# A semaphore for each of the 48 places of gathered rows in a message-passing kernel

## The chip, the cores and the metric

The kernel runs on one core of a Trainium2 chip. The metric is the device time of one execution in microseconds (us), lower is better; of several executions the median is given. A profiled execution gives a span, which runs from the first to the last instruction, and a trace of every instruction, DMA packet and semaphore event.

The engines are named as in the profile: PE is TensorE (PEld its weight loads), DVE is VectorE, ACT is ScalarE, POOL is GpSimd and SP is SyncE. A "q" behind a name (POOLq, DVEq, ACTq, SPq) is the engine's instruction queue, in which waits and DMA issues stand.

## The reference

There are 50,000 nodes with 160 features and 1,650,000 edges, sorted by their destination `dst`; `src` is in no order. For each edge the source node's row is fetched and combined with four numbers of the edge; the messages are summed at the destination, multiplied by small matrices, added to the node, and normalized:

```python
ss, vv = (s[src], v[src])                       # rows of x, by source
...
m = jnp.concatenate([out0, out1.reshape(-1, 3 * MUL1)], axis=1)
m_agg = jax.ops.segment_sum(m, dst, num_segments=n)
hs = m_agg[:, :MUL0] @ Ws * LIN_S
hv = jnp.einsum('nui,uw->nwi', m_agg[:, MUL0:].reshape(n, MUL1, 3), Wv) * LIN_V
h = jnp.concatenate([hs, hv.reshape(n, 3 * MUL1)], axis=1)
return x + jax.nn.relu(h)
...
x = _layernorm(x + _L0_gnn_ref(x, edge_attr_4, ...), axis=-1)
```

The messages are linear in the edge's numbers and in the source's row, so the kernel first sums the rows weighted by each of the four numbers and applies the merged matrices once for each node.

## The kernel before

**Units, groups, pairs, chunks.** 128 edges are a unit: one row of `x` (640 bytes) in each of the 128 partitions. Six units make a group (`G`), whose destinations lie within 32 neighbouring nodes; two groups make a pair (`PG`), so a pair has 12 units; 20 groups (`SG`), ten pairs, make a chunk. The main loop is written out over all 1,044 pairs.

**Fetching the rows.** The rows of a unit are fetched in one of two ways.

- Most come by an indirect DMA that POOL issues (line 468 in `gather`). It reads 128 row numbers, one column of the table `si`, and fetches the 128 rows into one of the 12 places of a tile `xg` (`rows[j]` is `xg[:, j, :]`). The pool `rowp` has four such tiles, 4 x 12 = 48 places, used in turn. POOL issues 12,230 of these gathers, in the order of the edges, and does next to nothing else.
- From the seventh chunk on ACT fetches the rows of two units in each chunk, and from the ninth on SP those of one (class `Fetcher`): 128 DMAs of one row each, into tiles `xscalar` and `xsync`. These DMAs increase a semaphore that the kernel itself allocates for the tile (`then_inc`), and the matmul that reads the tile waits for that semaphore by an explicit `wait_op`.

**What the matmuls do.** DVE makes a tile `ha` for each pair (line 486): for each edge of the pair its place among the 32 nodes, times its four numbers. PE then runs one matmul for each unit (line 511 in `group_sums`), `ha` by the fetched rows, and sums six units in `ps`. DVE turns the sums (line 527) and adds them into a ring of nodes (line 536). When a block of 128 nodes is complete PE multiplies it by the merged matrices (line 831) and DVE and ACT finish the nodes.

**What sets the order.** PE, DVE, ACT and SP run their instructions in the order in which the program is written; POOL's gathers are in the order of the pairs. The waits are put in by the framework that the kernel is written in. It knows which instruction writes and reads each tile. For the gathers it has eight semaphores, which the rows of the program call `DMASW0_49` to `DMASW7_49` (lanes, below): the gathers take them in turn, each adds 16 to its lane when it has landed, and before a gather takes a lane it waits until the lane's gather before, eight gathers earlier, has landed. The matmul of a unit waits for the lane of its gather. The first gather into a tile `xg` also waits for PE (`PE_49`), until the matmuls that read the tile's rows four tiles earlier are done, and at the start of a chunk for DVE (`DVE_49`), which writes the chunk's table `si` (line 426). That write in turn waits for all eight lanes, since older gathers read the table's buffer.

Of the kernel before, what the change touches and what calls it, by code (L numbers as in the profile page):

```python
# [67 lines left out]
PG = 2  # L68
# [16 lines left out]
def plan(n_nodes, n_edges):  # L85

    nblk = 125
    assert n_nodes % nblk == 0
    assert W == FB
    nb = n_nodes // nblk  # L90
    again = 9

    per_unit = P * n_nodes / n_edges
    group = max(g for g in range(1, 17)
                if g == 1 or (g + 0.2) * per_unit + 1 + 5 * math.sqrt(g * per_unit * per_unit / P) <= W)
    head = math.ceil(min(HEAD, n_edges / (group * P)) / SG) * SG
    eh = head * group * P
    row = group * P * 3 // 2 + math.floor(per_unit * group * 3 / 2 * (1 - n_nodes / n_edges))
    assert row * n_nodes / n_edges + 5 * math.sqrt(row * n_nodes / n_edges / 16) < KM

    far = math.ceil(6 * math.sqrt(n_edges) / 2 * n_nodes / n_edges) + 2
    rows = math.ceil((n_edges - eh) / row) + 2
    ngroups = math.ceil((n_edges - n_nodes + eh * n_nodes / n_edges + far) / (group * P))
    assert eh + (rows - 1) * row - n_nodes + eh * n_nodes / n_edges - far >= ngroups * group * P
    units = P * math.ceil(max(math.ceil(n_edges / P) + again - 1, math.ceil((eh + rows * row + 1) / P)) / P)
    return nblk, nb, again, group, units, ngroups, row, head, rows, far
# [3 lines left out]
def tile_gnn_resnorm(ctx: ExitStack, tc: tile.TileContext, x, src, dst, attr, W1, W2, W3, W4, W5, Ws, Wv, out, n_edges):  # L110
    nc = tc.nc
    N = x.shape[0]
    NBLK, NB, GA, G, NU, NG, L, NH, NR, FAR = plan(N, n_edges)
# [95 lines left out]
    def near(g):  # L209
        p = g * G * P  # L210
        return p / degree if p <= EH else EH / degree + (p - EH) / (degree - 1)
# [6 lines left out]
    for g0, g1 in parts:  # L218
        t = min((near(g) / N for g in range(g0, g1 + 1)), key=lambda t: abs(t - 0.5))
# [14 lines left out]
    with tc.tile_pool(name="once", bufs=1) as once, tc.tile_pool(name="raw", bufs=2) as rawp, \  # L234
# [182 lines left out]
        def place(cast_):  # L417
# [40 lines left out]
            begun.append(nc.vector.tensor_reduce(extremes[:, 1, s:s + 1], rel[:, :n], axis=AX.X, op=ALU.max))  # L458
            placed[s] = si, rel, pk[:, :, us]

        def gather(s, placed, u, n):

            xg = rowp.tile([P, PG * G, D], F32, name="xg")
            rows = [fetched.pop((s, u + j), None) for j in range(n)]
            for j in range(n):
                if rows[j] is None:
                    rows[j] = xg[:, j, :], None, None, None
                    nc.gpsimd.indirect_dma_start(  # L468
                        out=xg[:, j, :], out_offset=None, in_=x,
                        in_offset=bass.IndirectOffsetOnAxis(ap=placed[0][:, u + j:u + j + 1], axis=0))  # L470
            return rows

        idle, sent = [], []
# [22 lines left out]
        def fresh(kind):  # L496
            written[kind].append([])

        def wrote(kind, ins):
            ws = written[kind]  # L500
            for old in ws[-3] if len(ws) > 2 else []:
                tc.declare_no_dep(ins.ins, old, reason="its reader has waited for it")
            ws[-1].append(ins.ins)
            return ins

        def group_sums(p, rows, ha):

            ps = psA.tile([P, PG, D], F32, name="ps")
            fresh("ps")
            for j, (xr, sem, count, key) in enumerate(rows):  # L510
                mm = nc.tensor.matmul(ps[:, j // G, :], ha[:, j].rearrange("p k w -> p (k w)"), xr,  # L511
                                      start=j % G == 0, stop=j % G == G - 1)
                if key:
                    mm.wait_op(sem, count, "sem-ge")
                    tc.declare_no_dep(mm.ins, group=key, reason="their own semaphore is waited for")
                    tc.declare_fence(mm.ins, group=key)
                if j % G == 0:
                    wrote("ps", mm)
                else:
                    written["ps"][-1].append(mm.ins)  # L520
                yield ps
# [22 lines left out]
        def row_start(r):  # L544

            lo, hi = (math.floor(r * L * (1 - 1 / degree)) - 2 * FAR - 2, math.ceil(r * L * (1 - 1 / degree)) + 2 * FAR + 2)
            return (max(lo, 0), hi if r else 0), (max(math.floor((EH + r * L) / degree) - FAR - 2, 0),
                                                  math.ceil((EH + r * L) / degree) + FAR + 2)
# [234 lines left out]
        def own_blocks(k):  # L783

            if min((k + 1) * S, N) <= row_start(0)[1][0]:
                return []
            return [list(range(b, min(b + BP, nblocks))) for b in range(k * SB, min((k + 1) * SB, nblocks), BP)]
# [196 lines left out]
        for i in range(npacks):  # L984
# [3 lines left out]
            own = next((k for k in range(NSEG) if min((k + 1) * S, N) > row_start(i * RP)[1][0] and own_blocks(k)), NSEG - 1)  # L988
# [22 lines left out]
        for p, (s, g, ng) in enumerate(pairs):  # L1011
# [5 lines left out]
            if p % per == 0 and s + 1 < NSC:  # L1017
                after_pair(p + 1, do_cast, s + 1)
                after_pair(p + 2, do_place, s + 1)
                if s + 2 == NSC:  # L1020
                    after_pair(p + 4, examine_all)
                    after_pair(p + 6, read_flags)
            rows = gather(s, placed[s], (g - s * SG) * G, ng * G)
            for j, ps in enumerate(group_sums(p, rows, has.pop(p))):
                if j == 1 and turning:
                    turn_sums(*turning)
                    turning = None
                if j == 3 and p + 1 < len(pairs):
                    s1, g1, ng1 = pairs[p + 1]
                    has[p + 1] = spread(placed[s1], (g1 - s1 * SG) * G, ng1 * G)  # L1030
                work(1.0)
                if p % per == FBEGIN and not j:
                    begun_at = p
                    for f in fetchers:
                        f.begin(s)
                for f in fetchers:
                    if f.left:
                        f.deal((p - begun_at + (j + 1) / (ng * G)) / per)
                if packs and p >= START:
                    when = p + (j + 1) / (ng * G)  # L1040
                    todo = math.ceil(len(packs[0]) * min(1, (when - began) / max(1, due[0] - began)))
                    for step in packs[0][done:todo]:
                        if step:
                            step()
                    done = max(done, todo)
                    if done == len(packs[0]):
                        packs.pop(0), due.pop(0)
                        done, began = 0, when
# [35 lines left out]
    with tc.tile_pool(name="up", bufs=1) as up, tc.tile_pool(name="us", bufs=2) as us, tc.For_i(0, once_more, 1):  # L1084
# [3 lines left out]
        mm = up.tile([P, 2, JU], F32, name="mm")  # L1088
# [32 lines left out]
        f = up.tile([PB, CB], F32, name="f")  # L1121
# [12 lines left out]
    with tc.tile_pool(name="edges2", bufs=2) as ep, tc.tile_pool(name="ops2", bufs=2) as op, \  # L1134
            tc.tile_pool(name="node2", bufs=1) as np_, tc.tile_pool(name="psA2", bufs=2, space=PSUM) as psA, \
            tc.tile_pool(name="psF2", bufs=1, space=PSUM) as psF:
        with tc.For_i(0, blocks, 1) as b:
# [5 lines left out]
            with tc.For_i(u0, u1, GA) as u:  # L1143
# [10 lines left out]
                xg = op.tile([P, GA, D], F32, name="xg2")  # L1154
# [71 lines left out]
```

## Time and profile before

| | |
|---|---|
| median of 3 runs | 15441.45 us |
| the three runs | 15405.63, 15441.45, 15442.74 us |
| the profiled execution | 15404.57 us, its span 15402.8 us |
| granted TensorE clock, mean | 0.578 of full speed |
| busy: PE / PEld / DVE / ACT / POOL | 10200.3 / 6755.8 / 7650.5 / 171.3 / 11597.4 us |
| HBM traffic over the span | 87 GB/s |

How to read what follows. A row of a view of groups gives the line, the engine, the operation, what is written and read, and the count; then the busy time and the mean duration of one in ns; then the idle time of the engine just before these instructions, with what ended it. For an indirect DMA on POOL the busy time is that in which POOL generates the transfer's descriptors; the transfer itself runs later on the 16 DMA engines. "issue" means that the profile shows nothing that the engine waited for. A row of the timeline gives the start and the duration in us, then the same names, and in brackets the idle time before it.

### The profile page before, as it was taken

The page shows a single profiled execution, that of the slowest core. Times are in us where ns is not written, and L with a number is a line of the kernel's source. Part 1 is how long each engine was busy: PE and PEld are TensorE (multiplying, and loading weights), DVE is VectorE, ACT ScalarE, POOL GpSimd, SP SyncE. Part 2 cuts the span into 40 slices and gives each one's busy share as a digit, 9 for nine tenths or more (in the row PEclk, how much of TensorE's full clock was granted, in tenths as well). Part 3 has the DMA queues.
Part 4 walks back from the last instruction along what each step waited for, and adds up shares of the span by engine and source line. Part 5 has one row for each costly group of instructions (what it writes and reads, how often), then busy time and mean ns, then how long its engine had stood idle before and what let it go on. Part 6 is the DMA issues. An engine that isn't in the chain of part 4 may idle for free.

```text
span 15402.8 us, 171527 instructions
## 1 busy us (share of the span) xinstructions
PE 10200.3 (66%) x28971; PEld 6755.8 (44%) x28972; DVE 7650.5 (50%) x12616; ACT 171.3 (1%) x273; POOL 11597.4 (75%) x12243
## 2 busy tenths in 40 slices
PE   3666666666666666666666666666666666666666
PEld 3444444444444444444444444444444444444444
DVE  8455355445535543563465355445634553554333
ACT  0000000000000000000000000000000000000000
POOL 7777777777777777777777777777777777777777
PEclk6655555555555555555555555555555555555555
DMA  3333333333333333333333333333333333333333
GB/s 83 100 81 94 91 81 85 97 88 83 92 94 81 84 96 91 81 85 98 87 83 91 93 82 84 97 88 82 86 98 87 81 88 93 81 86 85 86 81 75
DMA packets 906388, 1346.70 MB, mean 87 GB/s; under 512 B 291294, under 2 KB 680162, under 8 KB 902614
## 3 DMA queue, kind: packets, MB, share of 16 engines
q0 software_dynamic: 587040, 1002.66, 27.9%
q1 hardware_dynamic: 266794, 315.98, 6.7%
q10 hardware_dynamic: 51440, 17.04, 0.6%
q14 instruction: 883, 7.23, 0.2%
q8 instruction: 231, 3.78, 0.1%
HBM read 1263.28 MB, written 71.42 MB: 87 GB/s over the span
## 4 chain that ended last, share of the span: by engine, by line
POOL 53%; issue 23%; DMA 19%; PE 5%; DVE 1%; POOLq 0%
POOL xg L468 53%; DMA xg<-in_x,si 19%; PE ps L511 4%; PE phb L831 0%; DVE ha L486 0%; DVE ring L822 0%; DVE ring L536 0%; DVE sums L527 0%; DVE xr L818 0%; DVE hot L483 0%; DVE prow L697 0%; DVE ring L781 0%; DVE pri L692 0%; DVE spots L590 0%; DVE marks L690 0%
## 5 line engine op out<-in xcount | busy, mean ns | idle before, releaser
L468 POOL DMA_INDIRECT xg<-in_x,si x12230 | 11593.9, 948 | 3782.0 <-issue 3511.0
L511 PE MATMUL ps<-xg,ha 128*128 128x160 f32 x24460 | 9452.6, 501 | 5187.1 <-DMA xg<-in_x,si 4721.5
L511 PEld LDWEIGHTS ps<-xg,ha 128*128 128x128 f32 x24460 | 5773.0, 292 | 8629.5 <-DMA xg<-in_x,si 7467.8
L527 DVE STREAM_TRANSPOSE sums<-ps 128x320 f32<-128x320 f32 x1044 | 536.4, 514 | 6840.4 <-PE ps L511 6817.2
L486 DVE TENSOR_TENSOR ha<-hot,pk 128x1536 f32<-128x1536 f32 x1044 | 1830.5, 1753 | 35.9
L831 PE MATMUL phb<-BWk,ring 128*128 128x160 f32 (+1 forms) x3910 | 1256.1, 418 | 0.0
L831 PEld LDWEIGHTS phb<-BWk,ring 128*128 128x128 f32 (+1 forms) x3910 | 1027.4, 296 | 0.0
L536 DVE TENSOR_TENSOR ring<-ring,sums 128x160 f32 x2087 | 684.6, 328 | 340.1 <-issue 203.6
L483 DVE TENSOR_TENSOR hot<-bank,rel 128x384 f32<-128x384 f32 x1044 | 573.4, 549 | 12.6 <-DMA xt<-in_x 10.8
L697 DVE COPY_PREDICATED prow<-marks,prow 128x2370 f32<-128x2370 int32 (+5 forms) x198 | 548.6, 2771 | 1.1
L822 DVE STREAM_TRANSPOSE ring<-xr 128x1280 f32<-128x1280 f32 x188 | 467.4, 2486 | 6.5
L697 DVE COPY_PREDICATED pra<-marks,pra 128x1580 f32<-128x1580 int32 (+5 forms) x198 | 377.0, 1904 | 0.0
L818 DVE TENSOR_TENSOR xr<-xr,bank 128x1280 f32<-128x1280 f32 x188 | 278.9, 1484 | 6.6 <-DVE bank L817 0.2
L186 DVE SCALAR_TENSOR_TENSOR y<-phb,xt 128x320 f32<-128x320 f32 x196 | 95.5, 487 | 240.6 <-PE phb L831 240.3
L196 ACT ACTIVATE rstd<-mv,eps_t 128x2 f32<-128x2 f32 x196 | 58.0, 296 | 14076.2 <-DVE mv L191 13455.5
L533 DVE TENSOR_TENSOR ring<-ring 128x196 f32<-128x196 f32 (+20 forms) x485 | 149.0, 373 | 1.8
L511 PE MATMUL ps<-xscalar,ha 128*128 128x160 f32 x392 | 140.4, 460 | 0.0
L202 DVE TENSOR_SCALAR o<-y,mv,rstd 128x160 f32<-128x160 f32 x391 | 131.3, 377 | 7.5
L694 DVE COPY_PREDICATED_SCALAR hit<-marks,none 128x395 int32 (+5 forms) x198 | 129.8, 656 | 7.0
L781 DVE MEMSET ring<- 128x1280 f32 (+1 forms) x98 | 119.3, 1218 | 22.6 <-issue 22.6
L190 DVE BATCH_NORM_STATS2 st<-y 128x6 f32<-128x160 f32 x391 | 121.7, 311 | 6.7
L695 DVE COPY_PREDICATED hit<-marks,pri 128x395 int32<-128x395 int32 (+5 forms) x198 | 118.2, 597 | 6.9
(352 smaller groups left out, 2173.6 us busy)
## 6 DMA issues: line engine op xcount, KB each, us to landing
xscalar<-in_x ACTq DMA_DIRECT2D x25088, 0.6 KB
xsync<-in_x SPq DMA_DIRECT2D x12288, 0.6 KB
xg<-in_x,si POOLq DMA_INDIRECT x12230
xr<-in_x SPq DMA_DIRECT2D x187, 640.0 KB
r<-edges SPq DMA_DIRECT2D x100, 384.0 KB
edges<-prow SPq DMA_DIRECT2D x1330, 27.8 KB
xt<-in_x SPq DMA_DIRECT2D x195, 160.0 KB
out<-o SPq DMA_DIRECT2D x195, 160.0 KB
```

What stands on the lines that cost most here:

```text
L202: nc.vector.tensor_scalar(o[:n, i], y[:n, i], mv[:n, i, 0:1], rstd[:n, i:i + 1], op0=ALU.subtract, op1=ALU.mult)
L468: nc.gpsimd.indirect_dma_start(out=xg[:, j, :], out_offset=None, in_=x, in_offset=bass.IndirectOffsetOnAxis(ap=placed[0][:, u + j:u + j + ...
L483: idle[:] = [nc.vector.tensor_tensor(hot[:, :n], slotsP[:, 0:W].unsqueeze(1).to_broadcast([P, n, W]), rel[:, u:u + n].unsqueeze(2).to_broa ...
L486: nc.vector.tensor_tensor(ha[:, :n], hot[:, :n].unsqueeze(2).to_broadcast([P, n, NK, W]), pk[:, :, u:u + n].rearrange("p k u -> p u k").un ...
L511: mm = nc.tensor.matmul(ps[:, j // G, :], ha[:, j].rearrange("p k w -> p (k w)"), xr, start=j % G == 0, stop=j % G == G - 1)
L527: nc.vector.transpose(at[:, :ng], ps[:, :ng].rearrange("p g (b f) -> p g b f", f=FB))
L533: nc.vector.tensor_tensor(ring[k][:, b, :past], ring[k][:, b, :past], ring[k - 1][:, b, S:S + past], op=ALU.add)
L536: nc.vector.tensor_tensor(here, here, at[:, i], op=ALU.add)
L697: nc.vector.copy_predicated(what[:n, a:e], mi[:, r].unsqueeze(2).to_broadcast([n, e - a, what.shape[2]]), what[:n, a + d:e + d])
L818: nc.vector.tensor_tensor(xr[:, :nq], xr[:, :nq], sumP[:, :nq].unsqueeze(2).to_broadcast([P, nq, D]), op=ALU.mult)
L822: nc.vector.transpose(ring[k][:, :, c0:c0 + nq * W].rearrange("p b (w q) -> p q b w", q=nq), xr[:, :nq].rearrange("p q (b f) -> p q b f", ...
L831: wrote("misc", nc.tensor.matmul(ph[:nb], ring[k][:, i, c0:c0 + nb], BWk[:, i, :], start=i == 0, stop=i == ND - 1))
```

## The change

Each of the 48 places gets a semaphore of its own, `filled0_0` to `filled3_11`. A gather adds 16 to the semaphore of its place when it has landed, is taken out of the framework's lanes (`no_tile_sem_insts`), and its matmul waits for that semaphore. The framework is told that this matmul needs no further wait for the gather (`declare_no_dep`) and that the gather is known to have landed once the matmul runs (`declare_fence`). ACT's and SP's rows had this arrangement before and keep it.

```diff
+        filled = [[tc.alloc_semaphore(f"filled{t}_{j}") for j in range(PG * G)] for t in range(4)]
+        gathers = [[0] * (PG * G) for t in range(4)]
+        begun_tiles = [0]
+
         def gather(s, placed, u, n):
 
             xg = rowp.tile([P, PG * G, D], F32, name="xg")
             rows = [fetched.pop((s, u + j), None) for j in range(n)]
+            t = begun_tiles[0] % 4
+            begun_tiles[0] += 1
             for j in range(n):
                 if rows[j] is None:
-                    rows[j] = xg[:, j, :], None, None, None
-                    nc.gpsimd.indirect_dma_start(
+                    part = nc.gpsimd.indirect_dma_start(
                         out=xg[:, j, :], out_offset=None, in_=x,
                         in_offset=bass.IndirectOffsetOnAxis(ap=placed[0][:, u + j:u + j + 1], axis=0))
+                    gathers[t][j] += 1
+                    key = f"gather{begun_tiles[0]}_{j}"
+                    part.then_inc(filled[t][j], 16)
+                    tc.no_tile_sem_insts.add(part.ins.name)
+                    tc.add_to_no_dep_group(key, part.ins)
+                    rows[j] = xg[:, j, :], filled[t][j], 16 * gathers[t][j], key
             return rows
...
-                if key:
-                    mm.wait_op(sem, count, "sem-ge")
-                    tc.declare_no_dep(mm.ins, group=key, reason="their own semaphore is waited for")
-                    tc.declare_fence(mm.ins, group=key)
+                mm.wait_op(sem, count, "sem-ge")
+                tc.declare_no_dep(mm.ins, group=key, reason="its own semaphore is waited for")
+                tc.declare_fence(mm.ins, group=key)
```

No instruction that computes or moves data is added, removed or reordered on any engine; the waits in front of them differ. Two places show it. Lines behind the edit carry higher numbers in the changed kernel: the gather of line 468 is line 473 there, the matmul of line 511 is line 522.

POOL in the middle of the program, the gathers into one tile `xg` from the first of a chunk on and the first of the next tile. Before:

```order
L468 DMA xg<-in_x,si 128x160 [waits DMASW3_49,DVE_49,PE_49]
L468 DMA xg<-in_x,si 128x160 [waits DMASW4_49]
L468 DMA xg<-in_x,si 128x160 [waits DMASW5_49]
L468 DMA xg<-in_x,si 128x160 [waits DMASW6_49]
L468 DMA xg<-in_x,si 128x160 [waits DMASW7_49]
L468 DMA xg<-in_x,si 128x160 [waits DMASW0_49]
L468 DMA xg<-in_x,si 128x160 [waits DMASW1_49]
L468 DMA xg<-in_x,si 128x160 [waits DMASW2_49]
L468 DMA xg<-in_x,si 128x160 [waits DMASW3_49]
L468 DMA xg<-in_x,si 128x160 [waits DMASW4_49]
L468 DMA xg<-in_x,si 128x160 [waits DMASW5_49]
L468 DMA xg<-in_x,si 128x160 [waits DMASW6_49]
```

The same place in the changed kernel (`x11` is eleven equal rows that follow each other):

```order
L473 DMA xg<-in_x,si 128x160 [waits DVE_49,PE_49]
L473 DMA xg<-in_x,si 128x160 x11
L473 DMA xg<-in_x,si 128x160 [waits PE_49]
L473 DMA xg<-in_x,si 128x160 x11
L473 DMA xg<-in_x,si 128x160 [waits PE_49]
```

Every wait for a lane is gone; the waits for PE at a tile's first gather and for DVE at a chunk's first gather stand where they stood, and each waits for the same matmul as before.

DVE in the middle of the program, where it writes the table `si` of a later chunk (`rel` and `extremes` belong to the same chunk). Before:

```order
L447 STREAM_TRANSPOSE pk<-r_24905 128x4x4x32
L426 TENSOR_SCALAR si<-bank 128x120 [waits DMASW4_49,DMASW5_49,DMASW3_49,DMASW6_49,DMASW2_49,DMASW7_49,DMASW1_49,DMASW0_49]
L453 SCALAR_TENSOR_TENSOR rel<-bank,baseB 128x120
L457 TENSOR_REDUCE extremes<-rel 128x1 [waits DVE_49]
L458 TENSOR_REDUCE extremes<-rel 128x1
```

And in the changed kernel:

```order
L447 STREAM_TRANSPOSE pk<-r_24905 128x4x4x32
L426 TENSOR_SCALAR si<-bank 128x120
L453 SCALAR_TENSOR_TENSOR rel<-bank,baseB 128x120
L457 TENSOR_REDUCE extremes<-rel 128x1 [waits DVE_49]
L458 TENSOR_REDUCE extremes<-rel 128x1
```

The wait for all eight lanes is gone here too.

## The prediction

> **What bounds the kernel now.** I read the page's chain of waits first, then the groups of POOL, then the view of line 468 alone. From the page, the chain that ended last:
>
> ```profile
> POOL 53%; issue 23%; DMA 19%; PE 5%; DVE 1%; POOLq 0%
> ```
>
> From the view of POOL's groups, and from the view of line 468 (duration as minimum/median/maximum in ns, first and last start in us; then idle time before it and its count, by what ended it):
>
> ```profile
> L468 POOL DMA_INDIRECT xg<-in_x,si x12230 | 11593.9, 948 | 3782.0 <-issue 3511.0 <-PE ps L511 137.6 <-DMA xg<-in_x,si 121.8
> ```
>
> ```profile
> L468 POOL DMA_INDIRECT xg<-in_x,si x12230: 940/946/2522, 5.7 to 15379.1; - x198
> L468 POOLq EVENT_SEMAPHORE  x1040: 17/17/43, 58.8 to 15365.4; - x174
> ...
>   issue: 3511.0, 11468
>   PE ps L511: 137.6, 445
>   DMA xg<-in_x,si: 121.8, 287
> ...
>   DVE si L426: 2.9, 1
> ```
>
> POOL's gathers run from 5.7 us to 15379.1 us of a span of 15402.8, so POOL sets the pace all along: 11593.9 busy and 3782.0 idle make 15375.9. What remains is 5.7 us ahead of the first gather, which the second figure holds in part, and some 23 behind the last. The chain's 19% of DMA is no such share to be won: such a piece bridges several gathers, while POOL generates the next ones.
>
> Is the idle time a wait that can go? The timeline of POOL at the start answers it. The second to the eighth gather wait for nothing in either program, since no lane has been used yet:
>
> ```profile
> 7.08 0.95 POOL L468 DMA_INDIRECT xg<-in_x,si  x1 [0.31 <-issue]
> 8.33 0.95 POOL L468 DMA_INDIRECT xg<-in_x,si  x1 [0.30 <-issue]
> ...
> 14.58 0.95 POOL L468 DMA_INDIRECT xg<-in_x,si  x1 [0.30 <-issue]
> 15.83 0.95 POOL L468 DMA_INDIRECT xg<-in_x,si  x1 [0.30 <-issue]
> 17.08 0.94 POOL L468 DMA_INDIRECT xg<-in_x,si  x1 [0.30 <-issue]
> ```
>
> From 7.08 to 17.08 are eight gathers, 1.250 us each, and the pitch is the same with no wait (to 14.58) and with a wait for a lane that is satisfied (from 15.83). So 0.946 of generation and about 0.304 of idle time are what a gather costs without any waiting: 12,230 x 1.250 = 15287.5, nearly the whole span. Only what exceeds this can be won.
>
> PE is no second bound. In the view of waits (total us, times, longest us):
>
> ```profile
> PE ps L511 <- DMA xg<-in_x,si: 4721.5, 7053, 6.9
> PEld ps L511 <- issue: 441.7, 168, 36.8
> DVE sums L527 <- PE ps L511: 6817.2, 902, 17.2
> ```
>
> PE waits 4721.5 us for gathers, and DVE 6817.2 for PE.
>
> **The change part by part.**
>
> *The waits for lanes on POOL (removed).* A gather that lands more than about eight pitches, 10.0 us, after its start holds up the gather eight places behind it. The timeline shows it in one place, PE's row being the matmul of the gather that started at 8390.37:
>
> ```profile
> 8390.37 0.95 POOL L468 DMA_INDIRECT xg<-in_x,si  x1 [0.30 <-issue]
> 8391.62 0.95 POOL L468 DMA_INDIRECT xg<-in_x,si  x1 [0.30 <-issue]
> ...
> 8399.12 0.95 POOL L468 DMA_INDIRECT xg<-in_x,si  x1 [0.30 <-issue]
> 8402.55 0.90 PE L511 MATMUL ps<-xg,ha 128*128 128x160 f32 x2 [3.61 <-DMA xg<-in_x,si]
> 8402.76 0.94 POOL L468 DMA_INDIRECT xg<-in_x,si  x1 [2.70 <-DMA xg<-in_x,si]
> 8404.18 0.94 POOL L468 DMA_INDIRECT xg<-in_x,si  x1 [0.47 <-DMA xg<-in_x,si]
> ```
>
> The gather of 8390.37 lands some 12.1 us later, PE starts at 8402.55, and POOL, eight gathers on, at 8402.76 after 2.70 us of idle time: 2.4 more than without a wait. No later work on POOL makes that up, so it counts in full.
>
> All such stalls together: the idle time of 3782.0, less 2.9 of the first gather (it waits for `si`), less 12,229 times the idle time that no wait explains. That last figure has two ends. With 0.304, from the pitch above, 3717.6 is taken off and 61.5 us are left. With 3511.0 / 11468 = 0.306, the mean of those that the profile puts to "issue", 3744.5 is taken off and 34.6 are left; this is too little, since a wait for two semaphores is often put down to "issue". I take the middle, 0.305: 3729.8 off, **49 us** left, with 35 and 62 as the ends. The stalls put to PE belong to it: 137.6 / 445 = 0.309 each, hardly over the rest.
>
> *What takes the wait's place.* POOL's next limit is the wait for PE at a tile's first gather. Behind it stand this tile's 11 other gathers and all later ones, and PE, then DVE, would wait for those. It binds only when PE is at least 36 gathers behind, 36 x 1.25 = 45 us. The longest landing in the chain is this one:
>
> ```profile
> 8391.62 12.31 DMA xg<-in_x,si
> ```
>
> 12.31 us are ten gathers, and the longest single wait of PE's weight loads is 36.8. I take 0; the upper bound is the old stall come back, the whole 49. PE gets the late rows when it got them before and waits for those behind them less, out of 4721.5 us of slack.
>
> *More transfers at once.* After a late landing about two more gathers stand in the DMA queue than eight (ten, as above). From the page, by queue: packets, MB, share of the engines' time:
>
> ```profile
> q0 software_dynamic: 587040, 1002.66, 27.9%
> ```
>
> The gathers use 27.9% of the DMA engines' time, so the extra ones drain about three times as fast as POOL makes new ones. 0 taken; the upper bound is the first rival below.
>
> *POOL's separate wait instructions.* About 930 of its 1,040 EVENT_SEMAPHORE go, as a tile's first gather now has one wait in place of two. They take 17 ns each, 16 us at most; but the mean idle time before a gather put to PE, mostly such first ones, is 0.309 against 0.306, 3 ns more, so 930 x 3 ns = 3 us, hidden in the 0.30 otherwise. I count 0.
>
> *The waits on DVE and PE.* DVE's waits at the write of `si`:
>
> ```profile
> L426 DVEq EVENT_SEMAPHORE  x412: 21/50/50, 247.1 to 15232.3; - x138
> ```
>
> 412 x 0.05 = 21 us of DVE's queue. It lies under DVE's 6817.2 us of waiting for PE; with that cover gone it would be 21 us. On PE every matmul still waits for exactly its own gather, as before, and each matmul group for DVE: 0.
>
> **The sum.** 15402.8 - 49 = 15353.8, and 1.8 for what lies around the span (15404.57 - 15402.8): **15355 us**. With the ends it is 15342 to 15370. The profiled execution is the fastest of the four: the runs shown are 15405.63, 15441.45 and 15442.74. The 36 us between the two kinds can be more stalls at the lanes (landings a little slower, with many near the limit of 10.0 us) or 3 ns more on each of 12,230 gathers (36.7 us). In the first case the change takes them too and every run comes to 15355; in the second, two runs in three would stay at 15441 - 49 = 15392. I forecast the first, since landings of 10 to 12 us against a limit of 10.0 mean that a small delay adds up quickly.
>
> **The rivals.**
>
> *Slower: a deeper queue makes generation slower.* POOL's slowest gathers, with what DVE did beside them:
>
> ```profile
> 68.46 1.61 DVE L573 SCALAR_TENSOR_TENSOR node<-at,node 1x1408 f32<-1x1408 f32 x1 [25.90 <-POOL at L570]
> 68.59 2.52 POOL L468 DMA_INDIRECT xg<-in_x,si  x1 [0.17 <-issue]
> 71.42 2.26 POOL L468 DMA_INDIRECT xg<-in_x,si  x1 [0.30 <-issue]
> 73.98 1.53 POOL L468 DMA_INDIRECT xg<-in_x,si  x1 [0.30 <-issue]
> 75.81 2.10 POOL L468 DMA_INDIRECT xg<-in_x,si  x1 [0.30 <-issue]
> 78.21 1.15 POOL L468 DMA_INDIRECT xg<-in_x,si  x1 [0.30 <-issue]
> ```
>
> They take 9.56 us for five, 0.97 more than usual for each. Were this the price of a gather issued with more than eight others under way, and were there as many of these as the 287 that the profile puts to DMA, it would cost 278 us and give 15355 + 278 = 15633. It ends above the median from (15441 - 15355) / 287 = 0.30 us for each, and beyond 0.3% of it (15488) from 0.46. Against it: the gathers up to 8399.12 above take 0.95 with eight under way, and the five stand beside long DVE operations of a table's set-up. [...]
>
> *No change: the lanes never bind in truth.* Then the stalls are the landings' own or something else's, and come back elsewhere: 15405 to 15441. For it: 3511.0 of the 3782.0 us are put to no wait at all, and only 287 gathers to DMA. Against it: 8402.76, 0.21 us behind PE's start on the same gather. [...]
>
> *Much faster: a gather without a wait issues sooner.* The row at 68.59 has 0.17 of idle time in place of 0.30; 12,230 x 0.13 = 1590 us would give 13765. Against it: the gathers from 8.33 to 14.58, without any wait, have 0.30; that of 68.59 follows another kind of instruction.
>
> **How the numbers follow.** The forecast (15342 to 15370) has 0.53; the forecast with the slower runs unmoved by stalls (about 15392) 0.16; no change 0.17; slower 0.10; much faster 0.04. A measurement of this kernel can tell about 0.3% from no change, 46 us of the median, which puts the line at 15395: the second case lies on it, and I give each side half. Faster is 0.53 + 0.08 + 0.04 = 0.65, the same 0.08 + 0.17 = 0.25, slower 0.10. The range, 15335 to 15430, holds the first two cases and two thirds of the third, 0.80.
>
> **What would show it.** In the changed kernel's view of the gather's line the idle time should be near 3733 us, with no gap over 0.35 us but at the first few gathers, and the generation still 946 ns in the median. The largest distance from a gather's start to its matmul should stay near 12 us. A mean generation above 0.97, or gaps that end with PE, would show the first rival or a new wait; an idle time still near 3780 the second. The forecast is wrong if the span falls by less than 35 us or more than 62.

## The result, and the profile after

The change makes the kernel faster by 0.26%: 15398.13 us is the median of ten runs (15365.33 to 15401.53), against 15438.7 us (15405.63 to 15442.74, ten runs) for the kernel before beside it, a ratio of 0.9974 with a 95% interval of 0.9964 to 0.9984. The profiled execution took 15365.33 us, its span is 15363.6 us; before it was 15404.57 and 15402.8. So the span fell by 39.2 us, where 49 were forecast, and the median by 40.6 us, where 86 were forecast (15441 to 15355): it lies 43 above the forecast.

From the view of POOL's groups of the changed kernel:

```profile
L473 POOL DMA_INDIRECT xg<-in_x,si x12230 | 11598.7, 948 | 3732.5 <-issue 3585.4 <-PE ps L522 133.0 <-DVE si L426 3.2
```

From the view of the gather's line (durations in ns, first and last start), and from the view of POOL's waits (total us, times, longest us):

```profile
L473 POOL DMA_INDIRECT xg<-in_x,si x12230: 942/946/2524, 6.0 to 15334.3; - x198
L473 POOLq EVENT_SEMAPHORE  x104: 17/17/17, 147.3 to 15267.8; - x104
```

```profile
POOL xg L473 <- issue: 3585.4, 11757, 0.3
POOL xg L473 <- PE ps L522: 133.0, 436, 0.3
POOL xg L473 <- DVE si L426: 3.2, 1, 3.2
```

The same view of waits before the change has:

```profile
POOL xg L468 <- issue: 3511.0, 11468, 1.9
POOL xg L468 <- DMA xg<-in_x,si: 121.8, 287, 2.7
```

The idle time fell from 3782.0 to 3732.5 us, and nothing longer than 0.3 us is left in it but the wait of the first gather; before, pieces of up to 1.9 and 2.7 us stood there. DMA is no longer named as what ended any of it. Generation is 946 ns in the median, as before.

The same late gathers as in the prediction's example, from the timeline of the changed kernel. The gather of 8389.58 lands 12.9 us later (by the semaphore events), the longest landing of this trace:

```profile
8389.58 1.04 POOL L473 DMA_INDIRECT xg<-in_x,si  x1 [0.30 <-issue]
8390.92 0.94 POOL L473 DMA_INDIRECT xg<-in_x,si  x1 [0.31 <-issue]
...
8399.67 0.95 POOL L473 DMA_INDIRECT xg<-in_x,si  x1 [0.30 <-issue]
8400.92 0.95 POOL L473 DMA_INDIRECT xg<-in_x,si  x1 [0.30 <-issue]
...
8402.55 2.77 PE L522 MATMUL ps<-xg,ha 128*128 128x160 f32 x6 [4.07 <-DMA xg<-in_x,si]
8403.42 0.95 POOL L473 DMA_INDIRECT xg<-in_x,si  x1 [0.30 <-issue]
```

PE waits for the late rows as it did, 4.07 us here, and POOL goes on at its pitch of 1.25 us. Before, the 2.70 us of idle time stood at this place.

Downstream little moved; from the view of waits:

```profile
DVE sums L537 <- PE ps L522: 6776.7, 901, 17.2
PE ps L522 <- DMA xg<-in_x,si: 4738.6, 7116, 6.6
PEld ps L522 <- issue: 300.4, 52, 36.9
```

PE now waits 4738.6 us for gathers (4721.5 before) and its weight loads 36.9 at the longest (36.8), DVE 6776.7 for PE (6817.2), less by about as much as the span. The gain arises on POOL.

**Where the rest of the 49 us went.** The end of the program holds it. POOL's queue at the line of the program's end, before and then after:

```profile
L1222 POOLq DRAIN  x3: 40/133/3340, 15398.5 to 15402.6; - x3
L1222 POOLq EVENT_SEMAPHORE_RANGE_CLEAR  x1: 285/285/285, 15402.2 to 15402.2; - x1
```

```profile
L1232 POOLq DRAIN  x3: 40/203/8975, 15353.3 to 15363.3; - x3
L1232 POOLq EVENT_SEMAPHORE_RANGE_CLEAR  x1: 545/545/545, 15362.7 to 15362.7; - x1
```

The longest of three DRAINs takes 8.975 us in place of 3.340, when the other engines are done: 5.6 us more. The account of the span: idle time 49.5 us less, generation 4.8 more (11598.7 for 11593.9), and from the last gather's end to the span's end 28.3 for 22.8, so 5.5 more. That is 39.2 less, which is what was measured.

### The profile page after: what moved, and what is told of

The parts are those of the page before. It is cut to its first block, busy times and chain, and to the rows that moved or that the text cites. A ratio compares the mean times of both kernels' runs of the same rounds, so it can differ in the third digit from the quotient of the medians.

```text
span 15363.6 us, 170159 instructions
## 1 busy us (share of the span) xinstructions
PE 10238.7 (67%) x28971; PEld 6764.9 (44%) x28972; DVE 7652.9 (50%) x12616; ACT 171.4 (1%) x273; POOL 11602.2 (76%) x12243
## 5 line engine op out<-in xcount | busy, mean ns | idle before, releaser
L473 POOL DMA_INDIRECT xg<-in_x,si x12230 | 11598.7, 948 | 3732.5 <-issue 3585.4
L522 PE MATMUL ps<-xg,ha 128*128 128x160 f32 x24460 | 9486.8, 503 | 5104.3 <-DMA xg<-in_x,si 4738.6
L537 DVE STREAM_TRANSPOSE sums<-ps 128x320 f32<-128x320 f32 x1044 | 536.3, 514 | 6789.7 <-PE ps L522 6776.7
```

The lines of the kernel that those rows point to most:

```text
L473: part = nc.gpsimd.indirect_dma_start(out=xg[:, j, :], out_offset=None, in_=x, in_offset=bass.IndirectOffsetOnAxis(ap=placed[0][:, u + j:u ...
L537: nc.vector.transpose(at[:, :ng], ps[:, :ng].rearrange("p g (b f) -> p g b f", f=FB))
```

## The experiments

Each run is compared with runs of the kernel before in the same session. In four later sessions that kernel took 15404 to 15411 us in the median; two others are named where they come.

**The change again.** The same kernel, in a later session.

> The changed kernel once more. Theory: the idle time of POOL in front of its gathers is again 3732 us within 2 (12,230 x 0.305), no gap over 0.35 us but the one behind the table's IOTA; profiled time 15365 within 5. The 33 us by which the timed executions (15398) stand above the profiled one (15365) come again, as they stand in the kernel before too (15439 and 15405), so they have nothing to do with the lanes. Rival, as the prediction had it: those 33 us are stalls at lanes; then the timed executions of this kernel, which has no lanes, should come to 15365 here and the ten runs so far were disturbed. Mean generation of a gather: 948.4 ns again if the 0.4 ns over the kernel before is the change's, back near 948.0 if it is chance.

Measured: 15361.9 us (15360.57 to 15363.32, eight runs) beside 15404.19 (twenty runs), ratio 0.9972 (0.9961 to 0.9982). The gain is 42 us again, and the 33 us between the profiled run and the other nine of the first session came in neither kernel, though the expectation's theory had them come again. They belong to that session, not to the change. The generation is 11595.3 us in this trace, against 11598.7 in the first one and 11593.9 before the change, so most of those 4.8 us more are not the change's.

**Lanes of the kernel's own.** To turn the number of gathers that may be under way as the one thing, the 48 places' semaphores are replaced by K semaphores used in turn, and each gather waits for the one K gathers back:

```diff
-        filled = [[tc.alloc_semaphore(f"filled{t}_{j}") for j in range(PG * G)] for t in range(4)]
-        gathers = [[0] * (PG * G) for t in range(4)]
-        begun_tiles = [0]
+        LANES = 8
+        filled = [tc.alloc_semaphore(f"lane{i}") for i in range(LANES)]
+        issued = [0]
...
-                    gathers[t][j] += 1
-                    key = f"gather{begun_tiles[0]}_{j}"
-                    part.then_inc(filled[t][j], 16)
+                    lane, before = issued[0] % LANES, issued[0] // LANES
+                    issued[0] += 1
+                    key = f"gather{issued[0]}"
+                    if before:
+                        part.wait_op(filled[lane], 16 * before, "sem-ge")
+                    part.then_inc(filled[lane], 16)
...
-                    rows[j] = xg[:, j, :], filled[t][j], 16 * gathers[t][j], key
+                    rows[j] = xg[:, j, :], filled[lane], 16 * (before + 1), key
```

> The changed kernel with eight semaphores of its own in place of 48, each gather waiting until the gather eight before it has landed, as the framework's lanes made it wait. Theory (the wait is all there is): back to the kernel before, idle time 3770 to 3785, profiled 15395 to 15406, ratio to the kernel before 0.999 to 1.001. Rival (the gain is from the rest of the edit: fewer wait instructions on POOL and DVE, other waits on PE): it stays at 0.997.

Measured with 8: 15394.11 us, ratio 0.9994 (0.9985 to 1.0003). From the views of POOL's groups and waits:

```profile
L471 POOL DMA_INDIRECT xg<-in_x,si x12230 | 11598.4, 948 | 3770.9 <-issue 3582.2 <-PE ps L523 107.6 <-DMA xg<-in_x,si 68.7
```

```profile
POOL xg L471 <- DMA xg<-in_x,si: 68.7, 125, 2.8
```

With a wait eight back the stalls of up to 2.8 us are there again, whoever owns the semaphores, and most of the gain is gone. Of the gain, 10 us stay; the idle times, 3770.9 here and 3782.0 before, differ by 11.1. The semaphore events of the two traces show where most of that lies. A gather that itself carries the wait for its lane starts 0.26 us after the landing that it waited for, in both. At a tile's first gather the kernel before waits for the lane by a separate instruction in front, since the gather carries the wait for PE; in 26 stalls at such places it starts 0.77 us or more after the landing. In e2 it is the other way round there: the separate instruction waits for PE, and the gather for its lane. These half microseconds sum to 8.8 of the 11.1 us.

The same edit with `LANES = 6`:

> Six such semaphores, six gathers or 7.5 us back. Theory: from the landing times in the changed kernel's trace (a quarter of them above 6.9 us, a tenth above 8.2) a wait six back adds 708 us of stalls if the landings stay as they are, against 37 for eight back; fewer under way may land sooner, so 400 to 750: ratio to the kernel before 1.023 to 1.047. Rival (late landings come from POOL's own depth of queue, so a shorter queue lands in time): within 0.5% of the kernel before.

```profile
L471 POOL DMA_INDIRECT xg<-in_x,si x12230 | 11595.5, 948 | 4263.5 <-issue 3337.0 <-DMA xg<-in_x,si 786.7 <-PE ps L523 112.5
```

Measured: 15885.44 us, 3.1% slower (1.0296 to 1.0328). The idle time is 4263.5, so 531 us more than in the changed kernel, and the generation is as before. Six lanes cost more than ten times what eight cost (38 us by e2's row), since many more gathers land between six and eight pitches: in the changed kernel's trace, by the semaphore events, 16% of them take 7.5 to 10.0 us, and 1.4% longer.

With `LANES = 10`:

> Ten semaphores, each gather waiting for the one ten before it, 12.5 us back. Theory: the landing times of the changed kernel's trace leave 0.6 us of stalls at ten back (37 at eight, 708 at six), so the idle time is 3731 to 3735; the DRAIN at the end should lie between that of eight (3.34) and of sixteen (6.44), near 4.3, so the kernel ends up to 4 us before the changed one. Rival: the gain needs the lanes gone altogether; then it lies midway between e2 (eight lanes) and the changed kernel.

```profile
L471 POOL DMA_INDIRECT xg<-in_x,si x12230 | 11596.4, 948 | 3732.5 <-issue 3602.2 <-PE ps L523 117.7 <-DVE si L426 3.0
```

Measured: 15358.01 us, ratio 0.9969 (0.9957 to 0.9980), idle time 3732.5: ten are enough. It is 4 us under the changed kernel of e1, and its DRAIN is 5.137 us (near 4.3 was expected), so 3.8 shorter than with 48.

With `LANES = 16`:

> Sixteen such semaphores, each gather waiting for the one sixteen before it, 20 us back. Theory: the longest landing seen is 12.9 us, so the wait never binds though every gather still has one: idle time 3732 again. At the end POOL's long DRAIN takes 8.97 us in the changed kernel and 3.34 before; if that is a price for each semaphore that gathers use (5.63 us / 48 = 0.117 us), it is 3.34 + 16 x 0.117 = 5.2 here, and the kernel ends some 4 us sooner than the changed one: profiled 15361, ratio 0.9971. Rival (a wait that stands on each gather costs something even when satisfied): idle time above 3740.

Measured: 15359.98 us, ratio 0.9971 (0.9959 to 0.9982), idle time 3734.8, DRAIN 6.443 (5.2 was expected from a price for each semaphore). Its profiled run alone took 15389.26 us, the other six 15356.93 to 15360.25, so this trace shows what a run that is 30 us longer looks like. From the view of POOL's groups, then that of the gather's line:

```profile
L471 POOL DMA_INDIRECT xg<-in_x,si x12230 | 11624.0, 950 | 3734.8 <-issue 3585.5 <-PE ps L523 140.0 <-DVE si L426 2.9
```

```profile
L471 POOL DMA_INDIRECT xg<-in_x,si x12230: 942/949/2519, 5.7 to 15361.9; - x198
```

The idle time is not longer. The generation is: 949 ns in the median for 946, and 11624.0 us in all, 27.6 more than with ten lanes (11596.4). What made this run longer is generation, not waiting.

**Twice the semaphores.** Two sets for the same 48 places, used alternately:

```diff
-        filled = [[tc.alloc_semaphore(f"filled{t}_{j}") for j in range(PG * G)] for t in range(4)]
-        gathers = [[0] * (PG * G) for t in range(4)]
+        SETS = 8
+        filled = [[tc.alloc_semaphore(f"filled{t}_{j}") for j in range(PG * G)] for t in range(SETS)]
+        gathers = [[0] * (PG * G) for t in range(SETS)]
...
-            t = begun_tiles[0] % 4
+            t = begun_tiles[0] % SETS
```

> The changed kernel with two semaphores for each place, used in turn by the uses of the place: 96 in place of 48. POOL's long DRAIN at the end took 2.20 us with 6 semaphores in use, 3.34 with 8, 6.44 with 16 and 8.97 with 48. Theory A: it grows with the semaphores in use, more slowly the more there are; then 9.0 to 12 us here. Theory B: it depends on how many of the last gathers have a semaphore that no later gather took, and reaches its end below 48; then 8.97 again and the whole within 2 us of the changed kernel. The gathers themselves: idle time 3731, no stall, either way.

Measured: 15362.65 us, ratio 0.9973 (0.9963 to 0.9983), DRAIN 8.975 to the digit as with 48. It does not grow any more.

**Half the places.** Two tiles `xg` instead of four, with 24 semaphores:

```diff
-            tc.tile_pool(name="idx", bufs=2) as idxp, tc.tile_pool(name="rows", bufs=4) as rowp, \
+            tc.tile_pool(name="idx", bufs=2) as idxp, tc.tile_pool(name="rows", bufs=2) as rowp, \
...
-        filled = [[tc.alloc_semaphore(f"filled{t}_{j}") for j in range(PG * G)] for t in range(4)]
-        gathers = [[0] * (PG * G) for t in range(4)]
+        SETS = 2
+        filled = [[tc.alloc_semaphore(f"filled{t}_{j}") for j in range(PG * G)] for t in range(SETS)]
+        gathers = [[0] * (PG * G) for t in range(SETS)]
...
-            t = begun_tiles[0] % 4
+            t = begun_tiles[0] % SETS
```

> The changed kernel with two tiles xg in place of four, 24 places and 24 semaphores. Theory: the wait for PE at a tile's first gather takes over when POOL may run only 12 to 24 gathers ahead. In the changed kernel's trace that wait is fulfilled 17 us ahead of need at the least and 40 us in the median; two tiles fewer take 30 us off, which leaves 18 of the 1,040 tiles late, 105 us in sum: ratio to the kernel before 1.002 to 1.006, the stalls ended by PE. With the four tiles it then had 17 us to spare everywhere, which is why nothing took the lanes' place. Rival: PE frees tiles so early that even two do not bind; then 0.997 as the changed kernel.

Measured: 15366.34 us, ratio 0.9975 (0.9966 to 0.9985). The expectation was too high. POOL's wait for PE:

```profile
POOL xg L474 <- PE ps L523: 132.3, 422, 4.0
```

There is one stall, of 4.0 us, some 106 us into the span. The tiles that had little room all lie in the first 650 us, and one stall delays POOL for all that follow; summing their shortfalls counted the same delay many times. The largest shortfall alone is 13.0 us. That 4.0 were enough goes with PE being earlier here: its one wait for DVE's `cum` in the set-up took 26.5 us, where it took 36.5 in the changed kernel. Why it was shorter isn't known. So the wait for PE, which took the place of the lanes, binds neither with 48 places nor, but for once, with 24.

**More units fetched as single rows.** POOL sets the pace, 1.25 us for each gather, so a unit that ACT or SP fetches is worth that, if they are in time. First two units by SP in each chunk in place of one:

```diff
-BY_SYNC, SYNC_FIRST = (1,), 8
+BY_SYNC, SYNC_FIRST = (2,), 8
```

> The changed kernel with SP fetching the rows of two units of a chunk in place of one, from the ninth chunk on; POOL issues 96 gathers fewer. Theory: with no stalls left POOL's 1.253 us for each gather is all that sets the pace, so 96 x 1.253 = 120 us go: ratio to the kernel before 0.989 to 0.990. Rival: SP's single rows (some 0.4 us each, 256 in 147 us beside its other transfers) come late, PE waits for them, and POOL in turn for PE's tiles: above 0.993.

Measured: 15702.45 us, 1.9% slower (1.0177 to 1.0211), with 12,134 gathers: the expectation's rival came. From the view of waits:

```profile
PE ps L522 <- DVE ha L497: 1779.9, 149, 77.3
DVE sa L826 <- DMA sa<-selves: 1609.0, 80, 85.0
PE ps L522 <- DMA xsync<-in_x: 630.0, 28, 57.0
POOL xg L473 <- PE ps L522: 532.2, 322, 43.6
```

SP is late with its rows and with its other loads (`sa`); PE waits up to 57 us for a unit, which is more than the 45 us that 48 places allow, and POOL stalls by up to 43.6 us. This is the wait for PE, seen binding.

With ten lanes and SP's second unit in every second chunk (`BY_SYNC = (1, 2)`):

> Ten lanes, and SP fetching one and two units in alternate chunks: 48 gathers fewer on POOL. In e8 two units in every chunk were too many for SP. Theory: in the mean SP has room for one and a half, and the four tiles let POOL run on over a late chunk: 48 x 1.253 = 60 us go from e6's 15358, to 15298, ratio to the kernel before 0.993. Rival: the chunk with two is late by itself, as in e8, and half of e8's loss comes: ratio above 1.000.

Measured: 15327.02 us, ratio 0.9945 (0.9928 to 0.9961), 29 us over the theory's 15298. The idle time is 3751.9 us, some 36 over 12,182 x 0.305, and POOL's longest wait for PE is 16.2; PE waits up to 46.2 us for SP's rows, so SP is still late at times.

In every fourth chunk (`(1, 1, 1, 2)`):

> The same with two units in every fourth chunk alone: 24 gathers fewer, 30 us, to 15328, ratio 0.995. Rival: each such chunk is late by some 7 us (e8 lost 340 us over 96 chunks, on top of the 120 it should have gained): 0.997 to 1.002.

Measured: 15335.06 us, ratio 0.9952 (0.9935 to 0.9969), DRAIN 3.177.

ACT's third unit in every second chunk, with ten lanes:

```diff
-BY_SCALAR, SCALAR_FIRST = (2,), 6
+BY_SCALAR, SCALAR_FIRST = (2, 3), 6
```

> Ten lanes, and ACT fetching two and three units in alternate chunks: 49 gathers fewer. ACT needs about 0.41 us for a row (140 in 56.8 us), so three units take 156 us of a chunk's 147, two 105, in the mean 131. Theory: the four tiles cover a chunk that is 10 us late, and 60 us go: 15298, ratio 0.993. Rival: ACT's short operations for the nodes stand behind its rows and hold up DVE: above 0.997.

```profile
L471 POOL DMA_INDIRECT xg<-in_x,si x12181 | 11553.1, 948 | 3718.6 <-issue 3596.3 <-PE ps L523 106.8 <-DVE ring L547 4.3
```

Measured: 15296.48 us (15295.8 to 15297.27), ratio 0.9927 (0.9911 to 0.9944), the fastest kernel of this study. 49 gathers fewer, no stall over 0.8 us, DRAIN 1.135.

Both, ACT's `(2, 3)` and SP's `(2, 1, 1, 1)`:

> e11's kernel with SP fetching a second unit in every fourth chunk too, in chunks in which ACT has two: 24 gathers fewer than e11. Theory: POOL's gathers alone set the pace, so the effects add: 15296 - 24 x 1.253 = 15266, ratio to the kernel before 0.991. Rival: ACT's and SP's heavier load meets in PE's waits; then no better than e11's 15296.

Measured: 23636.8 us, but the kernel before took 21048.96 beside it, 37% over its time in the other comparisons. Again, in another session:

> The kernel with ten semaphores, ScalarE's third unit in every second chunk and SyncE's second in every fourth, once more, since the kernel before took 21049 us beside it the last time. If that was the chip's condition and not the kernel: 12,157 gathers, 12206 - 12157 = 49 fewer than with SyncE's alone, so 15335 - 61 = 15274, or 15296 - 30 + a few us of late rows from SyncE = some 15270. If ScalarE's and SyncE's queues together are too slow for the rows: over 15300, with POOL's waits put to PE. DRAIN by theory R 7.668 again (the number of gathers is the same), whatever the time is.

Measured: 23434.91 us, and the kernel before 20909. Why both kernels were so slow in these two sessions isn't known (see the end), so what this version does where the kernel before takes its usual 15405 us stays open.

**What sets the DRAIN.** The kernels with ten lanes, 12,230, 12,206, 12,182 and 12,181 gathers, have 5.137, 3.177, 1.217 and 1.135 us, which does not go with the number of semaphores. The changed kernel with fewer gathers, by the edits above:

> The changed kernel with SyncE's second unit in every fourth chunk, so 24 gathers fewer (12,206). It tests what sets POOL's DRAIN at the end, the term that took back 5.6 us. Theory S (its length is set by the number of semaphores and levels off at 8.975 us): 8.975 again. Theory R (it is set by how many gathers are left over since some last clearing, whatever the number of semaphores; from the three kernels with ten semaphores, where 24 gathers fewer gave 5.137, 3.177 and 1 more gave 0.082: 0.0817 us for each gather): 8.975 - 24 x 0.0817 = 7.01. Under both the time is some 15336, near the same kernel with ten semaphores (15335).

> The changed kernel with ScalarE's third unit in every second chunk, 49 gathers fewer (12,181). Theory S: DRAIN 8.975. Theory R: 8.975 - 49 x 0.0817 = 4.97, unless a clearing comes between, when it is that and the length of one period more. POOL's idle time some 3717 (12,181 x 0.305 and no stall). Time by S 15362 - 49 x 1.25 = 15301, by R 15297; the same with ten semaphores took 15296.

The kernel before with ACT's `(2, 3)`:

> The kernel before with ScalarE's third unit in every second chunk, 12,181 gathers, on the framework's eight lanes. If the waits for lanes are worth the same 40 to 50 us here and more single rows do nothing else for them, 15405 - 61 = 15344, that is 48 above the same with ten semaphores (15296), with idle time near 12,181 x 0.305 + 45 = 3760. DRAIN by theory S 3.340 as before; by theory R 49 x 0.0817 = 4.00 us shorter than 3.340, which is below nothing, so a clearing has to come between and it is longer than 3.340.

The three ran in the session of e16 (21376.85, 23188.25 and 23203.9 us), so their times say nothing. The DRAIN doesn't depend on that: e12 and e16 have 7.668 both, of 12,157 gathers. e13 has 8.975; e14, then e15:

```profile
L1232 POOLq DRAIN  x3: 40/208/8893, 23176.5 to 23186.4; - x3
```

```profile
L1222 POOLq DRAIN  x3: 40/138/7995, 23185.5 to 23194.3; - x3
```

Both theories fell in part. All DRAINs are close to multiples of 0.0817 us (the 1.960 between 12,230 and 12,206 gathers, by 24), and with ten lanes one gather more, 12,182 for 12,181, gives one more (1.217 us for 1.135). That the lengths count gathers that are left over at the end is the author's estimate from these multiples, with ten lanes as with the others:

| semaphores | gathers | longest DRAIN, us | multiple of 0.0817 us |
|---|---|---|---|
| 6 | 12,230 | 2.197 | 27 |
| 8 | 12,230 / 12,181 | 3.340 / 7.995 | 41 / 98 |
| 10 | 12,157 / 12,181 / 12,182 / 12,206 / 12,230 | 7.668 / 1.135 / 1.217 / 3.177 / 5.137 | 94 / 14 / 15 / 39 / 63 |
| 16 | 12,230 | 6.443 | 79 |
| 24 | 12,230 | 9.220 | 113 |
| 48 | 12,134, 12,206 and 12,230 / 12,181 | 8.975 / 8.893 | 110 / 109 |
| 96 | 12,230 | 8.975 | 110 |

With eight or ten lanes the count lies between 14 and 98, and by this estimate it starts again at some point (with ten from 12,157 to 12,181 it falls by 80 where it should rise by 24, so after 104). With 48 or 96 it was 109 or 110 at every count that ran. What sets the count back, and why so differently, the traces don't show.

**The change with more single rows.** The two kernels with 12,181 gathers again, in a session in which the kernel before took 15407.86:

> The changed kernel with ScalarE's third unit in every second chunk once more, on another chip, since the kernel before took 20909 us beside it the last time. On a chip where that takes some 15405: POOL's idle time 12,181 x 0.305 = 3715 and no stall, DRAIN 8.893 again (the number of gathers is the same), so 15362 - 49 x 1.25 = 15301, some 4 above the same with ten semaphores (15296, DRAIN 1.135). If it is over 23000 again, the condition is not one of that chip.

> The kernel before with ScalarE's third unit in every second chunk once more: 12,181 gathers on the framework's eight lanes, DRAIN 7.995 again. If the waits for lanes are worth some 48 us of POOL's idle time here too: idle time near 3715 + 45 = 3760, and a time of 15405 - 61 + 4.7 (DRAIN 7.995 for 3.340) = 15349. Against e17 the change would then be worth 48 us and not 43, since its DRAIN is here only 0.9 us longer.

Measured: with the change 15302.08 us, ratio 0.9930 (0.9914 to 0.9947), as expected. Without it 15440.42, ratio 1.0021 (1.0012 to 1.0031): slower than the kernel before although it has 49 gathers fewer, and 91 over the expectation. The groups of e17, then of e18:

```profile
L473 POOL DMA_INDIRECT xg<-in_x,si x12181 | 11567.9, 950 | 3719.4 <-issue 3581.9 <-PE ps L522 124.8 <-PE phb L841 4.0
```

```profile
L468 POOL DMA_INDIRECT xg<-in_x,si x12181 | 11549.9, 948 | 3852.1 <-issue 3447.1 <-DMA xg<-in_x,si 259.4 <-PE ps L511 127.3
```

The stalls at the lanes are 132.7 us here (3852.1 less 3719.4), not 49. With ACT's additional rows the gathers landed later: by the semaphore events the median is 5.7 us and one in a hundred takes over 11.2 in e17, against 4.5 and 10.2 in the changed kernel; e11, with the same edit of ACT's units in another session, has 5.8 and 11.2. Eight back, 10.0 us, is then passed more often, by 5.3% of the gathers in e17 and 1.4% in the changed kernel. So the change is worth 138 us beside this other edit, and without it the edit loses time.

## Why the prediction was right and wrong

- **POOL sets the pace, and only what exceeds 1.250 us for each gather can be won: right.** The idle time is 3732.5, where 3733 was named as the sign, and the pitch is unchanged.
- **The waits for lanes are worth 49 us: right.** 49.5 were measured in the trace, and e2, e4, e6 and e3 turn them back on and off by the number of lanes alone: 3770.9, 4263.5, 3732.5 and 3734.8 us of idle time for 8, 6, 10 and 16. That the middle of 35 and 62 came within half a us is partly luck: 1 ns more or less before each gather, the distance from 0.305 to either end, moves it by 12 us. (12,229 x 3511.0 / 11468 is 3744.0, not 3744.5; the end of 35 stands.)
- **Nothing takes their place: right.** The wait for PE never binds with 48 places here (0.3 us at the longest), once with 24 (e7), and with late rows from SP (e8). DVE's waits for eight lanes were worth nothing that shows: DVE still waits 6776.7 us for PE. The separate wait instructions on POOL, 936 of which went, were counted as 0, and that is not quite so: they cost nothing where nothing stalled (305.0 ns of idle time before the gather in the mean, 304.9 before the others), but made 26 stalls longer, by 8.8 us in all (see e2), which are part of the 49.
- **The sum: a term was missing.** "1.8 for what lies around the span" and the 23 us behind the last gather were taken as unchanged. POOL's DRAIN there grew by 5.6 us. In the same kind of run the gain is therefore 39 to 43 us (39.2 by the spans, 42.3 in e1). This is no fixed price: with 12,181 gathers it is 0.9 (8.893 for 7.995).
- **The sum: the step that failed.** The prediction named two readings of the 36 us between the runs shown, and took the first, more stalls at the lanes in two runs of three, "since landings of 10 to 12 us against a limit of 10.0 mean that a small delay adds up quickly". So "every run comes to 15355". Nine of ten runs of the changed kernel, which has no lanes to stall at, took 15394 to 15402, 29 us and more over the profiled one, much as before the change. So the change took the 49 us of stalls and left the 36 us of the longer runs, where the forecast counted both. The second reading, 3 ns more on each gather, is what e3's trace shows in such a run (949 ns and 27.6 us in all; e17's profiled run, 20 us over its others, has 14.8 us more generation than e11's). That the runs of the first session were longer by the same is inferred from their size; none of the longer ones was traced. From the median the sum should have been 15441 - 49 = 15392, the second case, and 5.6 for the DRAIN: 15398. That this is the measured median to the digit is luck: from the ten runs' 15438.7 it is 15395. The premise, that a small delay adds up quickly, was not wrong in itself: in e18 the median landing is about 1 us later than before the change, and the stalls are 133 us. It was not what these longer runs had.
- **The rivals.** *Slower:* generation is flat with depth in the changed kernel's trace; its mean, by the number of gathers under way at the issue, is 948.1 ns with 2 or 5, 947.0 with 7, 950.2 with 8 and 944.8 with 9. The five slow gathers are still there, 2524 ns at most, with one other gather under way, beside the same DVE operations of the set-up (0.88 to 1.67 us each). That these made them slow was not shown: the gather behind them, of 79.91 us, takes 0.94 beside two of 1.53 and 1.51 us. *No change:* the stalls were the lanes' own, 121.8 us of idle time put to DMA before and none after, though the landings are as long: in the changed kernel 2.5 us at the shortest, 4.5 in the median and 12.9 at the longest, before 2.5, 4.4 and 12.3. *Much faster:* the idle time of 0.305 us before a gather without any wait stayed.

## What to carry to other kernels

Here eight completion semaphores used in turn let no more than eight transfers be under way, and the gather that landed 12.1 us after its start, longer than eight pitches of 1.25, cost POOL 2.4 us. Compare the tail of the landing times with the number of semaphores times the pitch of the issuing engine, and leave room: six lanes, 7.5 us back, cost 531 us of idle time here, eight 38 and ten none. Before a stall is priced by the spread between runs, ask which term of the sum differs in a long run: in the long run that was traced it was the 949 ns, for 946, of each of 12,230 gathers, not the waiting. And a change that is worth little alone may be what lets the next one pay: fetching more rows elsewhere lost 33 us with eight lanes (15440 for 15408) and won 60 with 48 semaphores (15302, for the 15362 of earlier sessions).

## What the runs showed of the hardware

- POOL's DRAIN at the end of the program takes 1.1 to 9.2 us in these kernels, 14 to 113 times 0.0817 us; with ten lanes each gather more added one such step. It begins some 18 us after the last gather, with the change (18.1) and without (18.5).
- A gather that carries its wait starts 0.26 us after the landing that it waited for; with the wait in a separate instruction in front, 0.77 us after it.
- The generation of a gather is 946 ns in the median before and after the change and in e1, e2, e4 to e8 and e11, and 949 in e3's trace. Its mean is 947 to 949 ns in all traces but e3's and e17's, 950, whose profiled runs took some 30 and 20 us more than the same kernel's others. In the traces before and after the change the first gather's first DMA packet starts 0.70 us after the end of its generation.
- In two sessions the kernel before took 20909 and 21049 us, and kernels with more single rows up to 23637. By the chip numbers on record one of the two chips is that on which e1 to e4 ran in the usual time. POOL's generation is the usual there (11523.1 us in e16), but POOL waits for PE, PE for DVE, and DVE for ACT:

```profile
POOL xg L471 <- PE ps L523: 6592.5, 440, 64.5
PE ps L523 <- DVE ha L498: 11056.9, 403, 84.4
DVE rstd L200 <- ACT rstd L196: 10108.6, 162, 105.6
```

ACT's `rstd` stands in ACT's queue among the single rows that ACT fetches, and these are slow to issue. The timelines from 1024 to 1040 us, e11 and then e14, with the same program on ACT:

```profile
1025.28 14.78 ACTq L381 DMA_DIRECT2D xscalar<-in_x  x38
```

```profile
1024.20 15.23 ACTq L381 DMA_DIRECT2D xscalar<-in_x  x15
```

ACT issues 38 of them in 14.78 us on the one and 15 in 15.23 on the other. In all of e14 its 31,360 rows run from 1024.2 to 23102.1 us, 0.70 us each, nearly the whole span. So by these rows ACT's queue, not POOL, sets the pace there; for ACT's rows themselves PE waits only 512.0 us in e16. Why the queue is slower isn't known. There 49 units moved from POOL to ACT made the kernel before 2295 us slower (e15, 23203.9 us for 20909), where the same move cost it 33 us in the usual time (e18).
